# Two attention layers on one core: even exponentials of the second layer summed by accumulating transfers, five split steps, projections in half blocks

## The chip, the cores and the metric

The kernel runs on one core of a Trainium2 chip. A core has five engines with queues of their own: PE (TensorE, matrix products into PSUM), DVE (VectorE) and ACT (ScalarE) for elementwise work, POOL (GpSimd) for elementwise work and for issuing DMAs, and SP (SyncE), which here issues DMAs only. The metric is the device time of one execution in microseconds; lower is better. Times named "profiled" come from one execution that the hardware profiler recorded.

## The reference

Input is `x` of 4 images, 64 x 64 positions, 256 channels, fp32. Each image is 4096 tokens. Two self-attention layers follow one another, both without scaling of the scores and both over the whole image:

```
layer 0:  q = x@Wq+bq  k = x@Wk+bk  v = x@Wv+bv        (32, 32, 256 wide)
          x = gamma * softmax(q k^T) v + x
layer 1:  f = x@Wf+bf  g = x@Wg+bg  v = x@Wh+bh        (32, 32, 128 wide)
          x = x + (softmax(g f^T) v) @ Wo + bo
```

All of it is fp32; the kernel keeps fp32-like accuracy while it runs most products in the faster rounded form (`fp32r`) with values that are split into a high and a low part.

## The kernel before

The kernel works image by image: layer 0 of an image ("first"), then its layer 1 ("second"). No scores are ever stored: exponentials are used as they come, and the division by their sum is done at the end of a block of queries.

**First layer.** 16 blocks of 256 queries; each goes in 8 steps over four key tiles of 128 keys. A step has four score products into the PSUM buffer `st` (L505), two exponentials on ACT, `high` (L515, with a small bias, rounded) and `p` (L517), then `low = p - high` on DVE (L522) and `d`, a combination of low and high (L527). `products_first` (L536) multiplies high, low and d by three prepared forms of v: 24 matmuls 258 wide, which also produce the sum of exponentials.

**Second layer.** Eight blocks of 512 queries; each goes in 16 steps over two key tiles. Scores are two products 512 wide (L505). Most steps multiply `p` with `v` in plain fp32 ("whole", L557, two products); the steps with `i % 5 == 2`, that is 2, 7 and 12, are split: high, low and d by three forms of v, six products in fp32r at L557. The sum of the exponentials is kept on DVE in `p_sum` (128 x 1024): a copy at step 0 (L696), an add in each of the 15 others (L698). At the end of a block `end_second` takes the result from PSUM to `o` (L613, L614), folds `p_sum` to `sums` (L616), and four `output` units do the product with Wo (L624), the sum over partitions (L625), the reciprocal (L627), scaling and residual (L628), and the store (L630).

**Order.** The main loop's iteration n issues the scores of step n+2, some small units of other work, then the products of step n. The program's order is a priority; a scheduler decides what stands where in each engine's queue, and tile pools decide when a buffer is free: one score buffer (two PSUM banks), four accumulators, two side banks. In SBUF `p` has three buffers, tag `t` (high, and p of the second layer's split steps) two, `l` two, `d` one (in the second layer it holds `p_sum`), q two, k eight.

**Projections.** One unit list per block of 512 tokens: `transpose_unit` (32 x 32 squares loaded by DMA, turned on DVE at L381, xh on ACT at L387, xl on DVE at L388), `qk_unit` (four products 512 wide at L412, ACT and DVE work at L422 to L425, and a store to `qk_dram` at L428), and `v_unit` (L442, then `split_values` at L400 to L403 or a plain copy at L463). `load_k` and `load_q` (L472) bring the rows of k and q back in the layout that the scores want, as four DMAs of 32 rows each, issued from POOL. The units are spread evenly over a block's steps; layer 1's projections of an image run during its layer 0, the last of them in the first block of its layer 1, and the next image's layer-0 projections run during layer 1. In the first image's first block projections run beside the steps as early units, three blocks ahead.

Of the kernel before, what the change touches and what calls it, by code (L numbers as in the profile page):

```python
# [55 lines left out]
P = 128  # L57
QB = 512
# [4 lines left out]
EPS = 2.0**-12  # L63
AHEAD = 3

# [168 lines left out]
def fast_path(ctx: ExitStack, tc: tile.TileContext, x, w0, w1, wo, bo, gamma, out, off):  # L234
# [13 lines left out]
    split = [[l == 0 or i % 5 == 2 for i in range(NI[l])] for l in range(2)]  # L248
# [11 lines left out]
    def wide(tag, name, dtype=F32):  # L260
        return work.tile([P, 2 * QB], dtype, tag=tag, bufs={"d": 1, "p": 3}.get(tag, 2), name=name)
# [5 lines left out]
    def load_squares(key, tokens):  # L267

        turned[key] = []
        for c in range(NCC):  # L270
            t = work.tile([P, QB], F32, tag="squares", bufs=5, name=f"squares_{key[0]}_{key[1]}_{key[2]}_{c}")
            for a in range(P // S):
                ch = c * P + a * S
                nc.sync.dma_start(
                    t[a * S : (a + 1) * S, :].rearrange("j (b i) -> j b i", i=S),
                    tokens[:, ch : ch + S].rearrange("(b j) i -> j b i", j=S),
                )
            turned[key].append(t)

    def load_block(b, j):  # L280
        if b < B and j < NB:
            load_squares((b, 0, j), x[b, j * QB : (j + 1) * QB, :])


    x_nat = {}

    def load_first(j):
        if j < NB:
            x_nat[j] = []
            for n in range(j * NT, (j + 1) * NT):  # L290
                x_nat[j].append(data.tile([P, C], F32, tag="v1", bufs=V1, name=f"x_nat_{n}"))
                nc.sync.dma_start(x_nat[j][-1], x[0, n * P : (n + 1) * P, :])

    load_first(0)
    load_first(1)

# [7 lines left out]
    seen_v = const.tile([P, 2, B * NB, 2], F32, name="seen_v")  # L304
# [61 lines left out]
    xT, x_parts, k_t, v_t = {}, {}, {}, {}  # L366
    qk_dram, x1_dram, x1_res = {}, {}, {}
    q_t = {}


    def transpose_unit(b, l, j):
        def issue():
            xT[b, l, j] = data.tile([P, NCC, QB], F32, tag="xT", name=f"xT_{b}_{l}_{j}")
            for c in range(NCC):
                if b == l == 0:
                    ps = side_psum(f"psx_{j}_{c}")
                    for t in range(NT):
                        nc.tensor.transpose(ps[:, t * P : (t + 1) * P], x_nat[j][t][:, c * P : (c + 1) * P], ident)
                    nc.scalar.copy(xT[b, l, j][:, c, :], ps)
                else:  # L380
                    nc.vector.transpose(xT[b, l, j][:, c, :], turned[b, l, j][c])  # L381
            x_parts[b, l, j] = []
            for c in range(NCC):
                parts = [
                    work.tile([P, QB], F32R, tag="squares", bufs=5, name=f"x{what}_{b}_{l}_{j}_{c}") for what in "hl"
                ]
                nc.scalar.copy(parts[0], xT[b, l, j][:, c, :])  # L387
                nc.vector.tensor_sub(parts[1], xT[b, l, j][:, c, :], parts[0].bitcast(F32))  # L388
                x_parts[b, l, j].append(parts)
            if b == l == 0:  # L390
                load_first(j + 2)
            elif l == 0:
                load_block(b, j + 1)
            elif j == NB - 1:
                load_block(b + 1, 0)

        return issue

    def split_values(v, h, low, d, seen):
        nc.scalar.activation(h, v, AF.Copy, scale=1.0 - DOWN)  # L400
        nc.scalar.activation(low, v, AF.Abs, accum_out=seen)
        nc.vector.scalar_tensor_tensor(d, h.bitcast(F32), -1.0 - EPS, v, ALU.mult, ALU.add)
        nc.vector.scalar_tensor_tensor(low, d.bitcast(F32), 1.0 / EPS, h.bitcast(F32), ALU.mult, ALU.add)  # L403

    def project_units(b, l, j):
        key = (b, l, j)

        def qk_unit():
            ps = side_psum(f"psqk_{b}_{l}_{j}")
            for c in range(NCC):  # L410
                for n in range(2):
                    nc.tensor.matmul(  # L412
                        ps,
                        wqk[l][:, c, :],
                        x_parts[key][c][n],
                        start=(c == n == 0),
                        stop=(c == NCC - 1 and n == 1),
                    )
            whole = data.tile([2 * D, QB], F32, tag="qk", name=f"qk_{b}_{l}_{j}")
            parts = data.tile([P, QB], F32R, tag="qk_parts", name=f"qk_parts_{b}_{l}_{j}")  # L420
# [6 lines left out]
            qk_dram[key] = dram.tile([2, 2, D, QB], F32, name=f"qk_dram_{b}_{l}_{j}")  # L427
            nc.sync.dma_start(qk_dram[key].rearrange("h w d n -> (h w d) n"), parts.bitcast(F32))  # L428
            if b == l == 0:
                near = parts.rearrange("(h w d) n -> h w d n", h=2, w=2)  # L430
                load_k(b, l, j, near)
                if j == 0:
                    load_q(b, l, j, near)

        per = QB // CV[l]

        def v_unit(t0):
            def issue():
                ps = side_psum(f"psv_{b}_{l}_{j}_{t0}").rearrange("p (t c) -> p t c", c=CV[l])
                for t in range(per):  # L440
                    for c in range(NCC):
                        nc.tensor.matmul(  # L442
                            ps[:, t, :],
                            xT[key][:, c, (t0 + t) * P : (t0 + t + 1) * P],
                            wv[l][:, c, :],
                            start=(c == 0),
                            stop=(c == NCC - 1),
                        )
                tiles = slice(t0, t0 + per)
                seen = [seen_v[:, l, b * NB + j, n : n + 1] for n in range(2)]  # L450
                if l == 0:
                    split_values(ps, *(v0[j][what][:, tiles, :C] for what in ("h", "l", "d")), seen[t0 // per])
                    return
                for n in range(NT // G[1]):
                    i = j * NT // G[1] + n
                    v = ps[:, n * G[1] : (n + 1) * G[1], :]
                    if split[1][i]:
                        t = data.tile([P, 3, G[1], P], F32R, tag="v1_parts", bufs=sum(split[1]), name=f"v_{b}_{i}")
                        v_t[b, i] = {what: t[:, m] for m, what in enumerate(("h", "l", "d"))}
                        split_values(v, *v_t[b, i].values(), seen[n])  # L460
                    else:
                        v_t[b, i] = data.tile([P, G[1], P], F32, tag="v1", bufs=V1, name=f"v_{b}_{i}")
                        nc.scalar.copy(v_t[b, i], v)  # L463
                        nc.scalar.activation(v, v, AF.Abs, accum_out=seen[n])  # L464

            return issue

        return [transpose_unit(b, l, j), qk_unit] + [v_unit(t0) for t0 in range(0, NT, per)]

    def load_rows(dst, parts, which, halves):  # L470
        for n, h in enumerate(halves):
            nc.gpsimd.dma_start(dst[n * D : (n + 1) * D, :], parts[h, which])  # L472

    def load_q(b, l, j, parts=None):
        q_t[b, l, j] = data.tile([P, QB], F32R, tag="q", bufs=2, name=f"q_{b}_{l}_{j}")
        load_rows(q_t[b, l, j], qk_dram[b, l, j].bitcast(F32R) if parts is None else parts, 0, (0, 0, 1, 1))

    def load_k(b, l, j, parts=None):
        k_t[b, l, j] = data.tile([P, QB], F32R, tag="k", bufs=NB, name=f"k_{b}_{l}_{j}")
        load_rows(k_t[b, l, j], qk_dram[b, l, j].bitcast(F32R) if parts is None else parts, 1, (0, 1, 0, 1))  # L480
# [8 lines left out]
    class Step:  # L489
# [8 lines left out]
        def scores(self):  # L498
# [18 lines left out]
            nc.scalar.activation(self.p, s_flat, AF.Exp)  # L517

# [5 lines left out]
        def cut_both(self):  # L524
            if self.split:
                self.d = wide("d" if self.l == 0 else "l", f"d_{self.key}", F32R)
                nc.vector.scalar_tensor_tensor(  # L527
                    self.d, self.low.bitcast(F32), -1.0 / EPS, self.high.bitcast(F32), ALU.mult, ALU.add
                )

# [13 lines left out]
        def products_second(self, acc):  # L544
            v = v_t[self.b, self.i]
            some = [i for i in range(NI[1]) if split[1][i]]
            for p, v, which, first, last in (
                (
                    (self.high, v["h"], 0, self.i == some[0], False),
                    (self.low, v["l"], 0, False, self.i == some[-1]),  # L550
                    (self.d, v["d"], 1, self.first, self.last),
                )
                if self.split
                else ((self.p, v, 1, self.first, self.last),)
            ):
                for g in range(G[1]):
                    nc.tensor.matmul(  # L557
                        acc[which],
                        v[:, g, :],
# [6 lines left out]
    def end_first(b, j, acc):  # L566
# [11 lines left out]
        def residual(s):  # L578
            def issue():
# [11 lines left out]
                if part == QB // QB0 - 1 and s == NS - 1:  # L591
                    load_squares((b, 1, jj), x1_dram[b, jj])
# [14 lines left out]
    def end_second(b, j, acc, p_sum):  # L607
# [7 lines left out]
        sums = work.tile([P, QB], F32, tag="sums", bufs=1, name=f"sums_{key}")  # L615
# [181 lines left out]
```

## Time and profile before

| What | us |
|---|---|
| median of 3 runs (3223.26 to 3223.58) | 3223.3 |
| the profiled execution | 3222.18 |
| its span (granted clock 0.998) | 3220.4 |
| first-layer block, without and with a projection | 26.9 and 29.6 |
| the first block of all | 67.2 |
| second layer, images 0 to 2: block 0; block 1; a later block | 51.0 to 52.7; 40.36; 41.75 |
| second layer, image 3: block 0; block 1; a later block | 45.05; 35.78; 37.17 |
| image 3's last block to the end of PE's work | 48.05 |

A block's time is the distance between the first score products of two blocks in the timeline of PE. The second layer of images 0 to 2 also carries the projections of the next image; image 3 has none to carry. Where a line of the profile names a line number, as L557, it is that of the kernel before; `acc<-p,v` means that `acc` is written from `p` and `v`.

### The profile page before, as it was taken

What the parts mean: (1) busy time and instruction counts of PE and PEld (TensorE: products, weight loads), DVE (VectorE), ACT (ScalarE), POOL (GpSimd) and SP (SyncE); (2) the same over time, 40 slices, a digit from 0 to 9 for tenths busy, and PEclk for the clock granted to TensorE, in tenths of its full rate; (3) what the DMA queues carried; (4) which work ended last, traced back from release to release, by engine and by line L of the source; (5) the groups of instructions that cost most, each with busy time, mean ns of one, the idle gap of its engine ahead of it and who ended that gap; (6) DMA issues with size and microseconds to landing.
All of it is one profiled execution on the core that took longest, in us unless ns stands there. A gap on an engine that the chain in (4) does not pass through costs nothing. (4 is left out here: it accounts for less than half of the span.)

```text
span 3220.4 us, 51144 instructions
## 1 busy us (share of the span) xinstructions
PE 3166.5 (98%) x19460; PEld 2613.0 (81%) x19460; DVE 2691.5 (84%) x3181; ACT 1988.8 (62%) x2483; POOL 661.3 (21%) x784
## 2 busy tenths in 40 slices
PE   8999999999999999999999999999999999999998
PEld 7999997566799999655679999966558999995554
DVE  7888888888888888788888888878888888887776
ACT  6666666655566666565556666655555666665554
POOL 3222223000232222200022222310002222241000
PEclk9999999999999999999999999999999999999999
DMA  4111123221212112322121112232222211121110
GB/s 120 47 47 44 50 50 83 56 53 49 59 44 54 44 52 49 79 53 53 49 64 42 49 50 50 61 70 52 51 52 57 53 41 47 46 70 47 36 36 31
DMA packets 368653, 172.16 MB, mean 53 GB/s; under 512 B 257392, under 2 KB 343664, under 8 KB 368400
## 3 DMA queue, kind: packets, MB, share of 16 engines
q1 hardware_dynamic: 342528, 134.29, 16.0%
q0 software_dynamic: 24960, 34.18, 4.5%
q8 instruction: 157, 2.57, 0.3%
q14 instruction: 96, 0.79, 0.1%
q10 hardware_dynamic: 912, 0.33, 0.0%
HBM read 99.22 MB, written 67.11 MB: 52 GB/s over the span
## 5 line engine op out<-in xcount | busy, mean ns | idle before, releaser
L517 ACT ACTIVATE p<-st 128x1024 f32<-128x1024 f32 x1024 | 1044.5, 1020 | 393.6 <-PE st L505 369.5
L515 ACT ACTIVATE high<-st,down 128x1024 fp32r<-128x1024 f32 x608 | 678.8, 1116 | 683.6 <-PE st L505 572.7
L527 DVE SCALAR_TENSOR_TENSOR d<-low,high 128x1024 fp32r<-128x1024 f32 x608 | 761.2, 1252 | 208.3 <-PE acc L536 202.9
L522 DVE TENSOR_TENSOR low<-p,high 128x1024 fp32r<-128x1024 f32 x608 | 810.6, 1333 | 134.2 <-ACT p L517 134.2
L557 PE MATMUL acc<-p,v 128*128 128x512 f32 x1664 | 795.2, 597 | 0.0
L505 PE MATMUL st<-q,k 128*128 128x256 f32 (+1 forms) x3072 | 778.6, 361 | 8.4 <-ACT p L517 8.3
L698 DVE TENSOR_TENSOR p_sum<-p_sum,p 128x1024 f32<-128x1024 f32 x480 | 587.1, 1223 | 60.7 <-ACT p L517 47.5
L505 PEld LDWEIGHTS st<-q,k 128*128 128x128 f32 x3072 | 461.2, 189 | 210.7 <-ACT p L517 113.3
L536 PE MATMUL acc<-v0d,d 128*128 128x258 f32 x4096 | 591.7, 284 | 1.7 <-DVE d L527 1.6
L536 PE MATMUL acc<-v0h,high 128*128 128x258 f32 x4096 | 588.6, 283 | 1.6 <-ACT high L515 1.6
L536 PE MATMUL acc<-v0l,low 128*128 128x258 f32 x4096 | 587.0, 283 | 0.5 <-DVE low L522 0.5
L536 PEld LDWEIGHTS acc<-v0d,d 128*128 128x128 f32 x4096 | 533.1, 189 | 6.7 <-DVE d L527 3.6
L536 PEld LDWEIGHTS acc<-v0h,high 128*128 128x128 f32 x4096 | 534.1, 190 | 3.4 <-ACT high L515 2.0
L536 PEld LDWEIGHTS acc<-v0l,low 128*128 128x128 f32 x4096 | 532.7, 189 | 0.8 <-DVE low L522 0.7
L557 PEld LDWEIGHTS acc<-p,v 128*128 128x128 f32 x1664 | 308.4, 190 | 214.3 <-issue 184.7
L593 POOL TENSOR_TENSOR x_res<-x,bo 128x256 f32<-128x256 f32 x128 | 216.3, 1690 | 889.9 <-DVE g L583 482.0
L472 POOL DMA_DIRECT2D q<-qk_dram x252 | 123.9, 501 | 1166.1 <-PE st L505 1143.0
L676 POOL TENSOR_TENSOR x_res<-x_res,bv 128x256 f32<-128x256 f32 x128 | 189.6, 1482 | 114.4 <-DMA x_res<-in_x 85.0
L442 PE MATMUL psv<-wv,xT 128*128 128x128 f32 (+1 forms) x1024 | 194.8, 331 | 6.8 <-DVE qk L423 6.1
L442 PEld LDWEIGHTS psv<-wv,xT 128*128 128x128 f32 x1024 | 159.6, 192 | 29.8 <-DVE qk L423 8.5
L472 POOL DMA_DIRECT2D k<-qk_dram x224 | 109.6, 500 | 245.2 <-PE st L505 140.3
L388 DVE TENSOR_TENSOR xl<-xT,xh 128x512 fp32r<-128x512 f32 x128 | 87.1, 683 | 5.1 <-ACT xh L387 4.7
(96 smaller groups left out, 1701.9 us busy)
## 6 DMA issues: line engine op xcount, KB each, us to landing
x_res<-in_x SPq DMA_DIRECT2D x128, 128.0 KB, 2.2
qk_dram<-qk_parts SPq DMA_DIRECT2D x64, 256.0 KB, 2.1
x_dram<-x SPq DMA_DIRECT2D x128, 128.0 KB, 1.7
x_res<-x_res SPq DMA_DIRECT2D x128, 128.0 KB, 1.7
squares<-x_dram SPq DMA_DIRECT2D x256, 64.0 KB, 2.3
x_old<-x_res SPq DMA_DIRECT2D x128, 128.0 KB, 2.0
out<-x_old SPq DMA_DIRECT2D x128, 128.0 KB, 1.7
q<-qk_dram POOLq DMA_DIRECT2D x252, 64.0 KB, 2.1
```

Of the source, the lines that this page charges most:

```text
L442: nc.tensor.matmul(ps[:, t, :], xT[key][:, c, (t0 + t) * P : (t0 + t + 1) * P], wv[l][:, c, :], start=(c == 0), stop=(c == NCC - 1),)
L472: nc.gpsimd.dma_start(dst[n * D : (n + 1) * D, :], parts[h, which])
L505: nc.tensor.matmul(st[:, g, :], k_t[b, l, kt // NT][:, kt % NT * P : (kt % NT + 1) * P], q_t[b, l, j * n // QB][:, q0 : q0 + n], start=Tru ...
L515: nc.scalar.activation(self.high, s_flat, AF.Exp, bias=down)
L517: nc.scalar.activation(self.p, s_flat, AF.Exp)
L522: nc.vector.tensor_sub(self.low, self.p, self.high.bitcast(F32))
L527: nc.vector.scalar_tensor_tensor(self.d, self.low.bitcast(F32), -1.0 / EPS, self.high.bitcast(F32), ALU.mult, ALU.add)
L536: nc.tensor.matmul(acc[2 * s + which][:, :W], p[:, g * QB0 + s * P : g * QB0 + (s + 1) * P], v0[self.i][v][:, g, :], start=self.first and ...
L557: nc.tensor.matmul(acc[which], v[:, g, :], p[:, g * QB : (g + 1) * QB], start=first and g == 0, stop=last and g == G[1] - 1,)
L593: nc.gpsimd.tensor_add(x_old[s], x_new[s], bo_sb)
L676: nc.gpsimd.tensor_add(x_res[b, j][t], x_res[b, j][t], bv)
L698: nc.vector.tensor_add(p_sum, p_sum, s.p)
```

## The change

Four things are done, all around the second layer and the projections:

1. `SPLIT1`: the second layer's split steps are 1, 4, 7, 10 and 13 (five of 16) instead of 2, 7 and 12.
2. `MOVED_SUMS`: the exponentials of the eight even steps are summed by DMAs that POOL issues. Step 0's p is copied into a tile `moved_sums` (tag `e`, one buffer), those of 2, 4, ... 14 are added to it by a DMA with `accum_op=add`; each DMA has 128 rows of 4096 bytes. DVE adds only odd steps (`add_up`; step 1 is a copy), and `end_second` adds `moved_sums` to `p_sum`.
3. Projections go by half blocks of 256 tokens: squares, xT, xh, xl, qk_parts are half as wide or hold both channel halves in one tile; psqk is four matmuls of 256 per half; each half is written to `qk_dram` by itself. In the first image's lead, xT, its parts and qk_parts share the five buffers of `v1_parts`, and k rows are loaded half by half.
4. `plan()` puts the units at given steps instead of an even spread: layer 1's halves in layer 0's blocks from 2 on, the last two halves at steps 0, 2, 3 and 6, 8, 9 of the second layer's block 0, the next image's halves seven steps apart.

`UP` is `1/EPS` as a constant. The core of the diff:

```diff
+SPLIT1 = (1, 4, 7, 10, 13)
+MOVED_SUMS = (0, 2, 4, 6, 8, 10, 12, 14)
...
-    split = [[l == 0 or i % 5 == 2 for i in range(NI[l])] for l in range(2)]
+    NH = N // QB0
+    split = [[l == 0 or i in SPLIT1 for i in range(NI[l])] for l in range(2)]
...
-        return work.tile([P, 2 * QB], dtype, tag=tag, bufs={"d": 1, "p": 3}.get(tag, 2), name=name)
+        return work.tile([P, 2 * QB], dtype, tag=tag, bufs={"d": 1, "e": 1, "p": 3}.get(tag, 2), name=name)
...
             self.p = wide("t" if self.split and l == 1 else "p", f"p_{self.key}")
             nc.scalar.activation(self.p, s_flat, AF.Exp)
+            if l == 1 and i in MOVED_SUMS:
+                if i == MOVED_SUMS[0]:
+                    moved_sums[b, j] = wide("e", f"p_sum_moved_{b}_{j}")
+                    nc.gpsimd.dma_start(moved_sums[b, j], self.p)
+                else:
+                    nc.gpsimd.dma_start(moved_sums[b, j], self.p, accum_op=ALU.add)
...
+        def add_up(self, p_sum):
+            if self.l == 0 or self.i in MOVED_SUMS:
+                return
+            if self.i == 1:
+                nc.vector.tensor_copy(p_sum, self.p)
+            else:
+                nc.vector.tensor_add(p_sum, p_sum, self.p)
...
         sums = work.tile([P, QB], F32, tag="sums", bufs=1, name=f"sums_{key}")
+        nc.vector.tensor_add(p_sum, p_sum, moved_sums[b, j])
         nc.vector.tensor_add(sums, p_sum[:, :QB], p_sum[:, QB:])
...
-        turned[key] = []
+        t = work.tile([P, NCC, QB0], F32, tag="squares", bufs=1, name="squares_" + "_".join(map(str, key)))
...
+            lead = b == l == 0
+            tag = "v1_parts" if lead else "xT"
+            xT[key] = data.tile([P, NCC, QB0], F32, tag=tag, bufs=LEAD_BUFS if lead else 1, name=f"xT_{b}_{l}_{h}")
...
+            if part == 0:
+                qk_dram[b, l, j] = dram.tile([2, 2, D, QB], F32, name=f"qk_dram_{b}_{l}_{j}")
+            nc.sync.dma_start(qk_dram[b, l, j].rearrange("h w d n -> (h w d) n")[:, cols], parts.bitcast(F32))
+            halves[b, l, j] = part + 1
...
+    def plan(b, l, j, ends):
+
+        units = {}
+
+        def put(i, *some):
+            units.setdefault(i, []).extend(some)
+
+        if l == 0:
+
+            if j >= 2:
+                t, qk, v = project_units(b, 1, j - 2)
+                put(0, t), put(4, qk), put(5, v)
+            for n, u in enumerate(ends):
+                put(1 + n, u)
+            return units
+        if j == 0:
+            for n, u in enumerate(ends):
+                put(1 + n, u)
+            for n, h in enumerate((NH - 2, NH - 1)):
+                t, qk, v = project_units(b, 1, h)
+                put(6 * n, t), put(6 * n + 2, qk), put(6 * n + 3, v)
+        else:
+            for n, u in enumerate(ends):
+                put(1 + n, u)
+        if b + 1 < B:
+            for h in range(NH):
+                i = 10 + 7 * h - j * NI[1]
+                for n, u in zip((0, 2, 3), project_units(b + 1, 0, h)):
+                    if 0 <= i + n < NI[1]:
+                        put(i + n, u)
+        return units
...
-        pace = NI[l] - (5 if l == 1 else 1)
-        upto = min(len(units), -(-len(units) * (s.i + 1) // pace))
-        todo = units[done:upto]
-        done = upto
+        s.add_up(p_sum)
+        todo = units.get(s.i, [])
...
-        while keys and keys[0] in qk_dram and (keys[0][:2] == (b, l) or keys[0][2] < over):
+        while keys and halves.get(keys[0]) == 2 and (keys[0][:2] == (b, l) or keys[0][2] < over):
             load_k(*keys.pop(0))
```

## The prediction

> **What bounds the kernel now.** I read the page first (busy shares, chain, groups), then the table of waits, then windows and timelines of single blocks of the second layer.
>
> ```profile
> PE 3166.5 (98%) x19460; PEld 2613.0 (81%) x19460; DVE 2691.5 (84%) x3181; ACT 1988.8 (62%) x2483; POOL 661.3 (21%) x784
> L557 PE MATMUL acc<-p,v 128*128 128x512 f32 x1664 | 795.2, 597 | 0.0
> L698 DVE TENSOR_TENSOR p_sum<-p_sum,p 128x1024 f32<-128x1024 f32 x480 | 587.1, 1223 | 60.7 <-ACT p L517 47.5
> k<-qk_dram POOLq DMA_DIRECT2D x224, 64.0 KB, 2.1
> ```
>
> TensorE (PE) is busy 98% of the span; VectorE (DVE) follows with 84%, 587 us of it the adds that this change halves. GpSimd (POOL) has room. So time goes only with PE work or with the few PE waits. The windows of three second-layer blocks (us, then busy PE, PEld, DVE, ACT, POOL, clock, DMA share, GB/s) show where the waits are: the first block of image 2, a later block of image 2, a block of image 3.
>
> ```profile
> 2107.60:2154.90 47.30, 41.62 (x134) 23.77 (x132) 36.85 (x43) 26.19 (x39) 5.47 (x6) 0.96 0.34 73
> 2237.00:2278.80 41.80, 41.55 (x141) 25.02 (x139) 35.52 (x44) 24.63 (x31) 2.01 (x5) 1.00 0.21 51
> 3015.70:3052.80 37.10, 36.79 (x119) 21.18 (x118) 29.19 (x34) 19.94 (x21) 1.88 (x5) 1.00 0.12 36
> ```
>
> Later blocks are full. The first block of an image has holes of 5.7 us, and its keys' load on POOL waits 23.43 us for the projection to reach memory:
>
> ```profile
> 2138.38 1.98 POOL L472 DMA_DIRECT2D k<-qk_dram  x4 [23.43 <-DMA qk_dram<-qk_parts]
> ...
> 2140.25 1.18 PE L557 MATMUL acc<-d,v 128*128 128x512 f32 x2 [1.54 <-DVE d L527]
> ...
> 2148.83 1.99 PE L442 MATMUL psv<-wv,xT 128*128 128x256 f32 x8 [1.84 <-DVE qk L423]
> ...
> 2153.00 0.72 PE L505 MATMUL st<-q,k 128*128 128x512 f32 x2 [1.71 <-ACT p L517]
> ```
>
> A split step is not free of waits either. Timeline of DVE and PE around step 12 of an image-3 block:
>
> ```profile
> 3046.94 1.22 DVE L522 TENSOR_TENSOR low<-p,high 128x1024 fp32r<-128x1024 f32 x1 [1.96 <-ACT p L517]
> 3048.09 1.22 DVE L698 TENSOR_TENSOR p_sum<-p_sum,p 128x1024 f32<-128x1024 f32 x1
> 3049.22 1.22 DVE L527 SCALAR_TENSOR_TENSOR d<-low,high 128x1024 fp32r<-128x1024 f32 x1
> ...
> 3050.49 0.73 PE L557 MATMUL acc<-d,v 128*128 128x512 f32 x2 [0.31 <-DVE d L527]
> ```
>
> An add sits between low and d and makes d late.
>
> **What the Trainium skill says.** "FP8 and Floating Point Precision", TensorE Precision Notes: true fp32 takes four passes. The trace agrees: successive unsplit steps start 2.18 us apart, 0.46 of it scores, so their two p·v matmuls take 1.72 us where two rounded ones of the same width take 0.46, a ratio of 3.7. "DMA: Bandwidth & Descriptors", Rules for kernel authors: an accumulating transfer is issued from GpSimd only, and another access to the same bytes waits for its semaphore; so the eight transfers of a block are a serial chain. No accumulating transfer is in the trace of before. "Collectives: The Full Stack", the bandwidth ceiling, says an add inside a transfer needs two reads for each write and so runs at about half a copy's rate; nothing here shows it.
>
> **The change part by part.** Sums start from the profiled execution, 3222.2 us (span 3220.4 plus 1.8 around it), 1.1 under the median of 3223.3.
>
> *Split steps.* Two more per block, 32 blocks: 64 steps. Unsplit: 2.18 us with scores; split: 8 x 0.23 = 1.845. So 64 x 0.335 = 21.4 us off PE. Not all arrives. An image-3 block takes 37.17 us (period between first scores); ideal is 13 x 2.18 + 3 x 1.845 + 2.28 (four output products of 0.57) = 36.16, so before loses 1.0, of it about 0.65 at step 12. The chain of a split step is scores, exp 1.11, exp 1.02, low 1.22, d 1.22: with hand-offs d is ready 5.25 us after the scores' start, 6.4 with an add between, and PE wants it at 5.8. After: 11 x 2.18 + 5 x 1.845 + 2.28 = 35.49. Odd steps keep their adds, and the compiled order on DVE still has add 7 and add 13 between low and d of steps 7 and 13. I put 0.5 at step 7, 1.35 at step 13 (d, and the single score buffer with two exponentials ahead of the last scores), 0.2 elsewhere: 37.5, that is +0.35 on an image-3 block. In images 0 to 2 a block has 41.75; ideal is 4.4 higher (3.46 psv + 0.96 psqk) and the projection's matmuls lie in the same holes, so I take 39.9 + 1.3 = 41.2: -0.55. 21 such blocks (two to eight) give -11.5, seven of image 3 +2.5.
>
> *The moved sums.* Seven adds and a copy leave DVE per block, one add of both sums comes in (L649 of after): net about -8 x 1.22 + 1.22 plus two lows and two ds, 4.9: DVE goes from 27.3 to 23.6 us per block. DVE isn't the bound, so this is worth only what waits it shortens. In place come 256 POOL transfers of 512 KB. Each waits for the one before. Their unknown cost T: k's 64 KB loads take 2.1 us from issue to landing with two packets of 0.1 per DMA engine, so 1.9 fixed; 512 KB is 8 rows of 4096 B per engine, at 159 ns per such packet on this queue 1.26, twice for two reads: T = 4.4. The skill's software path ("DMA: Bandwidth & Descriptors", Anatomy of one DMA) prices 2.0 us + bytes/436e3, an estimate of 4.4 for two reads, 3.2 for the copy. I take 4.6 with POOL's hand-off. Lower end 3.4 (reads of both operands side by side), upper end 6.5 (read, add and write one after the other). The block's chain is copy 3.2 + 7T + DVE's final add 1.6 = 37.0 at 4.6, against 37.5 and 41.2: it just fits, so I cost it at nothing in images 0 to 2 and 0 to 4 us in image 3. What hides it is that p has three buffers and each p's transfer has two steps (4.4 us or so) before its buffer is wanted. If the cover is gone ACT's exp waits (p of step 5 for transfer 0, high of 7 for transfer 4, and so on), then scores, then PE. Queued behind a waiting transfer on POOL are q's loads of a later block, which have a block to spare, in block 0 of an image the residual adds, and in block 7 k's loads for the next image.
>
> *Half blocks and fixed places.* Per projected block 8 psqk matmuls of 256 instead of 4 of 512: 0.96 instead of 0.93. Small DMAs double (squares, qk_dram; SP's queue has slack, transfers take 2 us and are issued half blocks ahead): nothing. What it buys is the start of a second-layer image: block 1's period and the projection taken away, block 0 of the four images loses 5.2 + 6.85 + 6.85 + 3.85 = 22.7 us against a steady one. After, only two halves remain for it, at steps 0 to 3 and 6 to 9 rather than to step 11, and the k rows of the last half are needed for scores of step 15 at step 13: ready 4 to 5 steps after qk at step 8, with 1 for projection chain, 2.1 for writing and 2.1 + 2 for loading. So I leave 1.6 each, 6.4, and gain 16; block 0's steady part moves by 3 x -0.55 + 0.35 = -1.3 like the others. Bounds: 8 to 20.
>
> *Start and end.* The first block of all takes 67.2 us against 26.9, of which PE's projections explain about 46. Now POOL issues 64 k loads of 0.5 us in it where it issued 32 (16 us more of a queue that gates the scores), and xT, its parts and qk_parts share a ring of five buffers; on the other side all work starts after half a block's input. I take +1, bounds -6 and +15. The end has one more DVE add in the tail, +1.2, and 2 for a transfer chain that lags in image 3.
>
> Sum: -11.5 + 2.5 - 16 - 1.3 + 1 + 1.2 + 2 = -22.1. That is a profiled execution of 3200.1; the median stood 1.1 higher, 3201.
>
> **The rivals.**
> A. The transfers are too slow (ends slower than before). The place is POOL's chain within a second-layer block, the price 8 us per block for each us of T (7 transfers and the copy), and it decides above T of about 5.1: there 7T + 4.8 = 40.5, +3.3 on the eight image-3 blocks (+27, which eats the -11.5 and -16) and nothing yet on the others. At T = 5.5 a block is 43.3: +1.5 on 24 blocks, +6 on eight, less the 16 to 18 at the starts: 3223 + 36 + 48 - 17 = 3290. At 6.5 it is 50.3: about +300. For it: no such transfer was measured here, each needs issue, landing and semaphore in series. Against it: POOL is 21% busy and its queue moves 4.5%.
> B. DVE, with 3.7 us less per block, gets d ready in time everywhere, so blocks come to 35.7 and 40.1: -1.65 on 24 and -1.5 on eight, -51, and -16 at the starts: about 3156. For it: low waits 134 us in all for p and adds fill those places. Against: add 7 and add 13 are still in between, and exp is the earlier link.
> C. Waits of the score buffer and d eat all of the split's gain (blocks +0.4 on both kinds, +13), the first block costs 8, and only part of the start stall goes (-16): within 0.2%, 3220.
>
> **How the numbers follow.** Forecast 0.50, A 0.33, B 0.10, C 0.07. The forecast's own range is 3182 to 3219 (starts 8 to 20, first block -6 to 15, blocks +-0.3). The range must reach into A: cut at T = 5.5 it leaves about a third to half of A out; below, 3165 leaves out B's better half. So 3165 to 3305. A measurement of this kernel can tell 0.2%, 6.4 us, from no change. Faster: forecast 0.49 and B 0.10, with little off for edges, 0.59; same 0.07; slower A 0.33 and a little of C, 0.34.
>
> **What would show it.** Accumulating transfers from issue to landing: under 5 us right, above A. Periods of 41.2 (images 0 to 2) and 37.5 (image 3); 39.1 or more there says A. DVE's add before sums waiting on a DMA for microseconds, and exp p waiting on a DMA, are A's marks. Block 0 of images 1 and 2 at about 46 instead of 52.6. d's waits at steps 7 and 13 on PE. First block 67 to 69. I am wrong if the transfers share their engines' time with the squares' small packets (16% of the queue share) and T varies, or if the half-block loads make k late at every start.

## The result and the profile after

The changed kernel takes 3330.4 us (median of 4 runs, 3327.6 to 3333.6) where the kernel before took 3223.4 beside it: a ratio of 1.033, 95% interval 1.032 to 1.035. It is slower by 107 us, outside the predicted range, and on the side of rival A. The page of the changed kernel, first part, then groups, then queues and DMA issues (issue to landing in us last):

```profile
PE 3195.1 (96%) x19844; PEld 2658.5 (80%) x19844; DVE 2605.9 (78%) x3229; ACT 2063.8 (62%) x2675; POOL 876.7 (26%) x1076
...
L545 POOL DMA_DIRECT2D p_sum_moved<-p x224 | 196.7, 878 | 942.0 <-ACT p L539 291.2
...
L649 DVE TENSOR_TENSOR p_sum<-p_sum,p_sum_moved 128x1024 f32<-128x1024 f32 x32 | 39.2, 1226 | 126.6 <-DMA p_sum_moved<-p 126.6
...
p_sum_moved<-p POOLq DMA_DIRECT2D x256, 512.0 KB, 4.9
```

The busy shares give no warning: PE went from 98% to 96%, DVE from 84% to 78%, ACT stays at 62%. POOL rose from 21% to 26%, which looks harmless. What gives it away is the group of L649: DVE's add of the two sums waits for the last transfer at the end of every one of 32 blocks, 126.6 us in all. The windows of one block of image 2 and two of image 3 (columns as before):

```profile
2278.10:2321.00 42.90, 42.56 (x153) 26.77 (x152) 31.90 (x44) 27.00 (x37) 8.48 (x12) 1.00 0.70 147
3089.90:3132.50 42.60, 38.07 (x124) 21.52 (x123) 25.54 (x31) 22.13 (x23) 8.63 (x12) 1.00 0.59 130
3132.50:3174.60 42.10, 38.08 (x124) 21.57 (x123) 25.58 (x31) 22.10 (x23) 8.62 (x12) 1.00 0.60 131
```

Image 3 is the clear case: 42.3 us a block for 38.1 of busy time on PE, where before it was 37.1 for 36.8. (By the prediction's own sum the products of a block fell from 36.2 to 35.5 us, so the 38.1 holds time in which PE was slowed too.) No engine fills the block, and the DMA engines are busy for only 0.60 of it. The block is a chain, and POOL's timeline shows it (start, duration, and in brackets the idle time ahead and what ended it):

```profile
3047.75 0.87 POOL L545 DMA_DIRECT2D p_sum_moved<-p  x1 [4.20 <-ACT p L539]
3048.28 2.33 POOL L490 DMA_DIRECT2D q<-qk_dram  x4
3054.81 0.56 POOL L543 DMA_DIRECT2D p_sum_moved<-p  x1 [4.19 <-ACT p L539]
3058.26 0.88 POOL L545 DMA_DIRECT2D p_sum_moved<-p  x1 [2.89 <-DMA p_sum_moved<-p]
3063.52 0.87 POOL L545 DMA_DIRECT2D p_sum_moved<-p  x1 [4.38 <-DMA p_sum_moved<-p]
3068.90 0.86 POOL L545 DMA_DIRECT2D p_sum_moved<-p  x1 [4.51 <-DMA p_sum_moved<-p]
3074.73 0.86 POOL L545 DMA_DIRECT2D p_sum_moved<-p  x1 [4.97 <-ACT p L539]
3080.16 0.86 POOL L545 DMA_DIRECT2D p_sum_moved<-p  x1 [4.57 <-ACT p L539]
3085.19 0.86 POOL L545 DMA_DIRECT2D p_sum_moved<-p  x1 [4.16 <-issue]
3090.25 0.86 POOL L545 DMA_DIRECT2D p_sum_moved<-p  x1 [4.20 <-ACT p L539]
```

From the copy at 3054.81 on, every issue follows its predecessor by 3.45 (the copy) and then 5.0 to 5.8 us, in all 35.4 to the last issue; the last transfer needs 5.5 more to land. In this case the releaser's name tells less than the distance: "ACT p" is the exponential that came last by the profile, in a step that was itself waiting. The landing is what counts: in the whole trace an accumulating transfer lands 4.9 us (median; 4.5 at the least) after its issue begins, and the next is issued 0.52 us (least; median 0.54) after that landing, so that from issue to issue the median is 5.4. The other end of the chain is on DVE:

```profile
3046.96 1.23 DVE L565 TENSOR_TENSOR p_sum<-p_sum,p 128x1024 f32<-128x1024 f32 x1 [0.20 <-ACT p L539]
3053.00 1.23 DVE L649 TENSOR_TENSOR p_sum<-p_sum,p_sum_moved 128x1024 f32<-128x1024 f32 x1 [4.82 <-DMA p_sum_moved<-p]
3054.26 0.69 DVE L650 TENSOR_TENSOR sums<-p_sum 128x512 f32<-128x512 f32 x1
3054.87 0.74 DVE L647 TENSOR_TENSOR o<-o,acc 128x256 f32<-128x256 f32 x2
3055.53 1.22 DVE L550 TENSOR_TENSOR low<-p,high 128x1024 fp32r<-128x1024 f32 x1
```

The transfer issued at 3047.75 lands just before 3053.0; DVE has stood still for 4.8 us, and only after L649 may the next block's copy overwrite the single `e` buffer, at 3054.81. Behind L649 in DVE's queue stands the next block's first `low`. So the chain closes over block borders, and it also reaches into the next image's first layer, where PE waits for that `low`:

```profile
881.44 1.34 PE L572 MATMUL acc<-v0l,low 128*128 128x258 f32 x8 [3.27 <-DVE low L550]
```

The spans differ by 105.4 us, and the distances between the first scores of blocks say where: second layer of images 0 to 2, +13.6, +15.2, +15.2; of image 3 up to PE's last product, +40.2; the first first-layer blocks of images 1 to 3, +15.1; the start, +4.2; the end after PE's last product, +1.8. These are 105.3 of the 105.4 us.

A part of it is a follow-up of the chain. In the profiled run the granted clock of PE was 0.5 in eleven stretches of 3.4 or 6.8 us, 48 us in all, the start and the end of the run aside; in the kernel before there were two, 6.8 us together. Each begins within 1.3 us of the end of a PE wait of 1.5 to 4.0 us. An estimate from these figures: up to half of the 41 us more, some 20 us of the loss, is PE at the lower clock after waits.

The long blocks of images 0 to 2 are blocks 4 and 7 (46.5 to 48.8 us; the other later blocks 42.2 to 45.5). The timeline of DVE and ACT at the start of image 0's block 4 shows a second way in which the chain holds them:

```profile
696.20 1.23 DVE L649 TENSOR_TENSOR p_sum<-p_sum,p_sum_moved 128x1024 f32<-128x1024 f32 x1 [4.17 <-DMA p_sum_moved<-p]
697.34 0.70 DVE L391 STREAM_TRANSPOSE xT<-squares 128x512 f32<-128x512 f32 x1
...
698.08 0.62 ACT L404 CAST xh<-xT 128x512 fp32r<-128x512 f32 x1 [4.62 <-DVE xT L391]
...
698.60 1.11 ACT L537 ACTIVATE high<-st,down 128x1024 fp32r<-128x1024 f32 x1
```

The next image's projection stands behind L649 on DVE, ACT waits for it, and the block's next exponentials stand behind that on ACT. Block 4 of images 1 and 2 looks the same, and in block 7 ACT waits 1.9 to 3.4 us for `qk` (L443), which stands behind L649 too. That this makes these blocks long is a reading of the timelines; no run changed it alone.

### The profile page after: what moved, and what is told of

It is laid out like the page before. It is cut to its first block, busy times and chain, and to the rows that moved or that the text cites. A ratio compares the mean times of both kernels' runs of the same rounds, so it can differ in the third digit from the quotient of the medians.

```text
span 3325.8 us, 53634 instructions
## 1 busy us (share of the span) xinstructions
PE 3195.1 (96%) x19844; PEld 2658.5 (80%) x19844; DVE 2605.9 (78%) x3229; ACT 2063.8 (62%) x2675; POOL 876.7 (26%) x1076
## 5 line engine op out<-in xcount | busy, mean ns | idle before, releaser
L537 ACT ACTIVATE high<-st,down 128x1024 fp32r<-128x1024 f32 x672 | 749.9, 1116 | 776.6 <-PE st L527 605.2
L550 DVE TENSOR_TENSOR low<-p,high 128x1024 fp32r<-128x1024 f32 x672 | 884.6, 1316 | 265.6 <-ACT p L539 265.0
L555 DVE SCALAR_TENSOR_TENSOR d<-low,high 128x1024 fp32r<-128x1024 f32 x672 | 849.0, 1263 | 186.7 <-PE acc L572 175.0
L527 PE MATMUL st<-q,k 128*128 128x256 f32 (+1 forms) x3072 | 740.0, 349 | 46.2 <-ACT p L539 35.5
L590 PE MATMUL acc<-p,v 128*128 128x512 f32 x1408 | 675.5, 601 | 0.0
L545 POOL DMA_DIRECT2D p_sum_moved<-p x224 | 196.7, 878 | 942.0 <-ACT p L539 291.2
L626 POOL TENSOR_TENSOR x_res<-x,bo 128x256 f32<-128x256 f32 x128 | 201.5, 1574 | 832.8 <-DVE x L618 829.7
L590 PEld LDWEIGHTS acc<-p,v 128*128 128x128 f32 x1408 | 261.3, 191 | 188.1 <-issue 165.6
L565 DVE TENSOR_TENSOR p_sum<-p_sum,p 128x1024 f32<-128x1024 f32 x224 | 273.2, 1219 | 19.8 <-ACT p L539 18.5
L649 DVE TENSOR_TENSOR p_sum<-p_sum,p_sum_moved 128x1024 f32<-128x1024 f32 x32 | 39.2, 1226 | 126.6 <-DMA p_sum_moved<-p 126.6
```

The costliest lines, as they stand in the source:

```text
L527: nc.tensor.matmul(st[:, g, :], k_t[b, l, kt // NT][:, kt % NT * P : (kt % NT + 1) * P], q_t[b, l, j * n // QB][:, q0 : q0 + n], start=Tru ...
L537: nc.scalar.activation(self.high, s_flat, AF.Exp, bias=down)
L545: nc.gpsimd.dma_start(moved_sums[b, j], self.p, accum_op=ALU.add)
L550: nc.vector.tensor_sub(self.low, self.p, self.high.bitcast(F32))
L555: nc.vector.scalar_tensor_tensor(self.d, self.low.bitcast(F32), -UP, self.high.bitcast(F32), ALU.mult, ALU.add)
L565: nc.vector.tensor_add(p_sum, p_sum, self.p)
```

## Experiments

Times are medians; the kernel before, run beside them, had 3222.5 to 3223.9. "A block" is a block of image 3 in the steady state unless said otherwise: 37.17 us before, about 42.3 in the changed kernel.

**All sums back on DVE.** `add_up` copies at step 0, and the add of the moved sum goes.

```diff
-MOVED_SUMS = (0, 2, 4, 6, 8, 10, 12, 14)
+MOVED_SUMS = ()
```

> The changed kernel with all 16 sums of a block back on DVE, everything else kept. Transfer chain (a block's period in the second layer is 7 times 5.2 to 5.6 us plus the copy and DVE's final add): without it image-3 blocks fall from 42.5 to about 37.5, the others from 43 to 47 down to about 41.2, the first first-layer block of images 1 to 3 from 34.3 to 29.5; 3195 to 3215 us in all. Split waits (five split steps with one score buffer and late d hold the blocks): blocks stay above 42, 3290 or more. Traffic (the moved bytes slow the engines' SBUF accesses): the same 3195 to 3215, so this run does not tell it from the chain.

3217.6 us, ratio 0.998 (0.9975 to 0.9993), just above the 3195 to 3215 that the chain would give. A block takes 38.03, blocks of images 0 to 2 41.0 to 42.7, the first first-layer block of images 1 to 3 29.1 (34.2 to 35.0 with the transfers). So the transfers cost 113 us, and the rest of the change is worth 6, not the 25 that I had summed for it (the sum of -22.1 has 3.2 of loss in it for the moved sums). Split waits as the main cause are out.

**Copies in place of adds.** The same 256 transfers in the same chain, without the add.

```diff
-                    nc.gpsimd.dma_start(moved_sums[b, j], self.p, accum_op=ALU.add)
+                    nc.gpsimd.dma_start(moved_sums[b, j], self.p)
```

> All eight transfers of a block are plain copies into the same tile, one after the other, so the tile ends up with the last even step's exponentials only and the even steps' sum is left out; issues, waits and written bytes stay. Transfer chain: a copy takes 2.9 us to landing and 0.53 to the next issue, 8 x 3.4 = 27 us, hidden under a block of 37 or 41; image-3 blocks about 37.3, in all 3185 to 3210. Split waits: stays at about 3320. Traffic: a third of the bytes (one of two reads) is gone, so about a third of the loss: about 3290.

3212.7 us, 3 above the chain's span. The DMA view of this kernel:

```profile
p_sum_moved<-p POOLq DMA_DIRECT2D x256, 512.0 KB, 3.0
```

8 x (3.0 + 0.5) = 28 us goes under any block, and the whole loss is gone although issues, waits and written bytes are all there. The chain is borne out; traffic, which should have kept two thirds of the loss, is not. But the adds themselves are gone too, and POOL is held 0.53 us for an issue instead of 0.87, so the next two runs, which keep adds, are needed beside this one. A block took 38.3, a us above the expected 37.3, as in the run before: that is the splits' share (below).

**Half-wide transfers, two chains.**

```diff
+                for g in range(2):
+                    cols = self.p[:, g * QB : (g + 1) * QB]
...
+                        nc.gpsimd.dma_start(moved_sums[b, j, g], cols, accum_op=ALU.add)
```

> Each moved sum is two transfers of half the columns into two tiles, so two chains of 256 KB transfers run side by side; same bytes and work, twice the issues. If T is mostly fixed latency (about 2 us plus 0.5 of hand-off, the rest by size), a half transfer lands in about 3.5, the chain is about 8 x 4 = 32 us and hidden: 3200 to 3225. If T is the engines' rate for the bytes, both halves together take what one took, 4.9, and two issues of 0.87 each come on top: 3330 or more. Split waits: 3330.

3233.4 us, much nearer to the fixed-latency value, 8 us above its end. The least time of an accumulating transfer fell from 4.5 to 3.25 us, of the copy from 2.86 to 2.26. If time grows in line with size, 4.5 - 3.25 = 1.25 for half the bytes makes 2.5 us by size and 2.0 fixed for a whole one. In the run the median of the half adds was 4.0, so part of the gain is lost; where two meet is the likely place. All adds and all bytes are still there, and all but 16 us of the 113 are gone: this is the strongest run against traffic.

**Four moved sums.** `MOVED_SUMS = (0, 4, 8, 12)`.

> Only steps 0, 4, 8 and 12 are moved, DVE adds the other twelve. Transfer chain: copy 3.4 + 3 x 5.5 + 1.6 = 21.5 us, well hidden under a block: 3195 to 3215, the same as with all sums on DVE or a few us less. Traffic: half of the loss remains, about 3265. Split waits: 3310 or more.

3211.6 us, as the chain says; with three of seven accumulating transfers kept, none of the loss is. A block takes 37.98: four sums fewer on DVE, with one add back at the end, are worth next to nothing against all 16 (38.03).

**Nine moved sums.** `MOVED_SUMS` with 15 added: the suspected cost enlarged.

> Step 15's sum is moved too, a ninth transfer at the end of each block. Transfer chain: it lengthens the chain of 32 blocks by one T of 5.3 to 5.5, less the DVE add of 1.2 that goes: 32 x 4.3 to 5.5, so 3465 to 3505 us. If the blocks were held by splits or by traffic, one transfer more costs at most 32 x 0.6 or so: about 3350.

3490.5 us (two runs): +160 for 32 transfers, 5.0 us each, inside the expected span. This is the price of one more link of the chain.

These runs settle the slowdown. The next ones ask why the rest gained 6 us only, and what five splits are worth.

**Three splits, sums on DVE.** Split steps 2, 7, 12 as before the change; the lead keeps its five buffers.

```diff
-SPLIT1 = (1, 4, 7, 10, 13)
+SPLIT1 = (2, 7, 12)
```

> All sums on DVE and the split steps 2, 7, 12 as in the kernel before; half blocks, fixed places and the five-buffer lead of the changed kernel stay. With five splits and sums on DVE the median was 3217.6, an image-3 block 38.04. If two more splits cost time instead of saving it (late d or score buffer): image-3 blocks about 37.2, in all 3195 to 3212. If five splits do save part of their 21 us: 3220 to 3235. Either way block 0 of images 1 and 2 at 43 to 46, which is what the half blocks bring.

3217.9 us and a block of 38.03: the same as with five. So the 64 further split steps brought nothing; and with the same split steps as the kernel before, a block is 0.86 longer. Neither expectation foresaw both. In this kernel's timeline of DVE and PE both later split steps (7 and 12) show the late `d` that the kernel before had at step 12 only:

```profile
3062.29 1.22 DVE L565 TENSOR_TENSOR p_sum<-p_sum,p 128x1024 f32<-128x1024 f32 x1
3063.43 1.22 DVE L555 SCALAR_TENSOR_TENSOR d<-low,high 128x1024 fp32r<-128x1024 f32 x1
...
3064.70 0.74 PE L590 MATMUL acc<-d,v 128*128 128x512 f32 x2 [0.32 <-DVE d L555]
...
3075.93 0.73 PE L590 MATMUL acc<-d,v 128*128 128x512 f32 x2 [0.32 <-DVE d L555]
```

The kernel before had an output product (0.57 us of PE) between the splits' scores and their products, since its units were spread over the block; at its step 12, whose `d` was late, there was none. `plan()` puts all four at steps 1 to 4. That this makes the 0.86 is a reading of the two timelines; with three splits it was not run.

**Four splits, sums on DVE.** `SPLIT1 = (1, 5, 9, 13)`.

> All sums on DVE, four split steps 1, 5, 9, 13. Score buffer: four steps need 3 x 1.85 + 2.8 = 8.35 us of the buffer against PE's 3 x 2.18 + 1.845 = 8.39, so PE can just follow; image-3 blocks 36.7 to 37.1 and about 3190 to 3200. Late d: one late d of about 0.65 per split, 4 x 0.65 over an ideal of 35.83, 38.4 at most, 37.5 at least, 3205 to 3220.

3210.5 us, a block 37.69: inside the span of late d, above that of the score buffer. Taken alone it speaks for late d as the limit; the next run shows that this isn't enough.

**The splits' own sums moved.** The add that stands between low and d is that of the split step itself, so moving just those takes it away.

```diff
-MOVED_SUMS = (0, 2, 4, 6, 8, 10, 12, 14)
+MOVED_SUMS = (1, 4, 7, 10, 13)
```

> The five split steps' own sums (1, 4, 7, 10, 13) are the moved ones, so no add stands between low and d on DVE; 3.4 + 4 x 5.5 = 25 us of chain, hidden. With four moved sums the second half of an image-3 block ran at 6.89 us per three steps, 0.35 of it PE's wait for d. Late d (the add between low and d costs the split's gain): the wait goes, three steps take 6.2 to 6.35, an image-3 block 36.3, in all about 3165 to 3180. Score buffer (one buffer, emptied by two exponentials in a split step, 1.85 + 1.85 + 2.8 = 6.5 per three steps, more than PE's 6.2): three steps stay at 6.5 to 6.7, a block at 37.0 to 37.5, 3190 to 3200.

3203.8 us, ratio 0.994 (0.993 to 0.996). The profile shows no wait of PE for d any more (about 1.0 us a block with four moved sums), yet three steps take 6.7 to 6.8 us (6.89 before) and a block 37.47, not 36.3. Late d accounts for about 0.5 us of a block; something else is nearly as late. The block lies in the score buffer's span, the total 4 us above it.

**High from p.** In the second layer p is exponentiated first, and high made from p, not from the scores.

```diff
             if self.split:
                 self.high = wide("t", f"high_{self.key}", F32R)
-                nc.scalar.activation(self.high, s_flat, AF.Exp, bias=down)
+                if l == 0:
+                    nc.scalar.activation(self.high, s_flat, AF.Exp, bias=down)
             self.p = wide("t" if self.split and l == 1 else "p", f"p_{self.key}")
             nc.scalar.activation(self.p, s_flat, AF.Exp)
+            if self.split and l == 1:
+                nc.scalar.activation(self.high, self.p, AF.Copy, scale=1.0 - DOWN)
```

> The split steps' own sums are moved, and in the second layer p is exponentiated first and high is made from p in SBUF, so that the score buffer is free after one exponential in every step. With own sums moved alone the median was 3203.8, three steps took 6.83 us and an image-3 block 37.47. Score buffer: 3 x 1.85 = 5.6 us is now under PE's 6.2, so three steps take 6.2 to 6.4 and an image-3 block 35.8 to 36.3, images 0 to 2 at 40 to 40.6; 32 blocks by 1.2 make about 3165. Late high and d: high comes 1.1 us later, low and d with it, and PE waits for them in the score buffer's place; three steps stay at 6.8 or more, 3200 or more.

With the own sums moved: 3199.0 us, a block 37.30 and three steps 6.7; the expected 36.3 was missed by a us. PE's timeline of this kernel:

```profile
3051.16 0.62 PE L593 MATMUL acc<-low,v 128*128 128x512 f32 x2
3051.97 0.49 PE L527 MATMUL st<-q,k 128*128 128x512 f32 x1 [0.19 <-ACT p L540]
3052.30 0.65 PE L593 MATMUL acc<-d,v 128*128 128x512 f32 x2
```

The scores now stand ahead of d in most split steps and wait for the exponential of the step before. That one waits for its own scores in the one buffer, and these for an exponential that stands right behind `high` in ACT's queue. And d is later than it was. DVE's timeline:

```profile
3048.67 1.22 DVE L553 TENSOR_TENSOR low<-p,high 128x1024 fp32r<-128x1024 f32 x1 [2.07 <-ACT high L542]
3049.82 1.22 DVE L568 TENSOR_TENSOR p_sum<-p_sum,p 128x1024 f32<-128x1024 f32 x1
3050.95 1.22 DVE L558 SCALAR_TENSOR_TENSOR d<-low,high 128x1024 fp32r<-128x1024 f32 x1
```

An add, that of the next step, is between low and d again. At steps 7, 10 and 13 of an image-3 block d is ready 6.3 to 6.9 us after the step's scores start, where the run with own sums moved had 5.3 to 5.7. The rival expectation, late high and d, is nearer to this run than the score buffer is.

> All sums on DVE and high made from p, so that only the score buffer's hold is changed against the run with sums on DVE (3217.6 us, image-3 block 38.04). Score buffer alone as the limit: 36.5 or less a block, about 3170. Late d: the add stays between low and d, and high is 1.1 us later, so PE's wait for d grows from 0.35 to about 1 a split step; 38.0 to 39.5 a block, 3215 to 3250.

With all sums on DVE: 3199.2 us, ratio 0.992 (0.990 to 0.994); a block 36.77, that is 1.27 below the same kernel with high from the scores. The total fell by 18 us, less than half of the 47 that the score buffer alone should have brought. The expectation for late d doesn't hold as it was put, for the edit changed DVE's order as well (step 10 of an image-3 block):

```profile
3053.55 1.23 DVE L568 TENSOR_TENSOR p_sum<-p_sum,p 128x1024 f32<-128x1024 f32 x1 [0.54 <-ACT p L540]
3054.69 1.22 DVE L553 TENSOR_TENSOR low<-p,high 128x1024 fp32r<-128x1024 f32 x1
3056.02 1.23 DVE L558 SCALAR_TENSOR_TENSOR d<-low,high 128x1024 fp32r<-128x1024 f32 x1
```

The split step's own add needs only p and now goes ahead of low. At some split steps the next step's add comes between low and d in its place, at this one none does. So at steps 7, 10 and 13 d is ready 5.5 to 6.7 us after the scores' start, against 6.3 to 6.7 with high from the scores: no later. The run therefore says nothing against late d. What the two runs show together is that the same edit brings 1.27 a block where d comes no later and 0.17 where d comes about 1.2 us later. That fits a limit of two parts, the hold of the score buffer and d, but no run changed the buffer alone.

**A ring of six in the lead.** Sums on DVE, `LEAD_BUFS = 6`.

> All sums on DVE, and the ring that the first image's projections share has six buffers instead of five. With five the first block took 80.3 us and the median was 3217.6. Ring as the limit of the start: the first block falls to 68 to 74, in all 3205 to 3212. Small pieces as the limit (hand-offs of 16 half blocks one after the other): it stays at 78 to 82 and 3215 to 3220.

3214.8 us against 3217.6. The first block takes 74.1 instead of 80.3, but begins at 22.1 instead of 17.6 us: the end of the first block comes 1.7 earlier. The ring matters to the first block's length and hardly to the whole; neither expectation held in full.

**Outputs at the split steps.** Sums on DVE, high from p, and in blocks 1 to 7 of an image:

```diff
             for n, u in enumerate(ends):
-                put(1 + n, u)
+                put(1 + 3 * n, u)
```

> All sums on DVE, high made from p, and a block's four output units at the split steps 1, 4, 7, 10 instead of steps 1 to 4 (blocks 1 to 7 of an image). Against 3199.2 us and an image-3 block of 36.77 with the outputs at steps 1 to 4. Bunching theory (an output product beside a split step gives high, low and d the time they lack; steps 7, 10 and 13 had none, which is also why three splits with fixed places took 38.03 a block where the kernel before, with its spread units, took 37.17): 36.0 to 36.4 a block, 28 blocks by 0.4 to 0.7, so 3179 to 3188. If the places of the outputs don't matter: 36.7 to 36.8, 3197 to 3201.

3183.8 us, ratio 0.9875 (0.986 to 0.989), a block 36.20, both inside the expected spans. The places of the outputs matter, and this version is the fastest of all, about 1.2% below the kernel before: it has the half blocks and five splits of the change, high made from p, and no accumulating transfer.

## Why the prediction was wrong

The step that failed is "The moved sums": "T = 4.4 ... I take 4.6 with POOL's hand-off ... it just fits, so I cost it at nothing" in images 0 to 2, with 2 us in the sum for image 3. The mechanism, a serial chain, was named rightly; its link was sized at 4.6 us and measured 5.4 (median from issue to issue), so that the chain did not fit under a block and cost 113 us.

- **T.** The transfer itself was estimated well: 1.9 fixed and 2.5 by size against 2.0 and 2.5 by the half-wide run, 4.4 against a least time of 4.5. The sum left out two things: the median is 4.9, not 4.5 (other traffic is a likely reason, not a tried one), and from landing to the next issue 0.52 us pass where I gave 0.2. Seven times the missing 0.8 is 5.6 us of a chain that had 0.5 to spare in image 3 and 4.2 in the others.
- **The point of decision.** I wrote that rival A decides above 5.1. That held, and so did its formula for a block: 7 x 5.4 + 4.8 = 42.6 for image 3, measured 42.3. Its marks are all there: besides DVE's 126.6 us before L649, ACT's exponentials wait 60.5 us in all for `p_sum_moved`. The price that I put beside it, 8 us a block per us of T, doesn't follow from the formula, which gives 7. A term with so steep a price and an estimate half a us below its edge should not have been the likeliest case; the choice of the value inside its bounds was the error, not the list of bounds.
- **Rival A's 3290 at T = 5.5** was 40 us short. Its own terms make about 23 us for the second layer of images 0 to 2 and 44 for image 3; measured are 44 and 40. It left out the projection's hold on ACT and DVE in blocks 4 and 7, L649's hold on the next image's first layer (+15), the start (+4) and the end (+2).
- **The skill's half rate for an add.** One packet of 4096 bytes took 161 ns (median) in the copies of step 0 and 338 in the adds, so just under half the rate. "Collectives: The Full Stack", the bandwidth ceiling, says it of a reduction between cores; inside this core the trace agrees.
- **Split steps: -11.5 in images 0 to 2 and +2.5 in image 3.** With sums on DVE these blocks did not gain: 0.2 us longer each over blocks 1 to 7 of image 1, and 0.87 longer in image 3. The parts named (d, the score buffer) were right in kind as far as the runs tell, their size was not. In the kernel before three split steps took (37.17 - 13 x 2.18 - 2.28) / 3 = 2.18 us each on average, just what a whole step takes, so a saving of 0.335 per step was not being realised even there; I had read the lost 1.0 us mostly as a fault of step 12.
- **Add 7 and add 13 between low and d.** True of the order, but with the own sums moved a block is only 0.5 shorter than with four other sums moved.
- **Fixed places.** I gave the bunching of the outputs no cost. It cost 0.57 a block with high from p (36.77 to 36.20), as much as the 0.5 that I put at step 7.
- **Image starts: -16.** With sums on DVE block 0 came to 43.5 in images 0 to 2 (51.0 to 52.7 before) and 42.7 in image 3 (45.05), 28 us in all, of which 4.4 came back in block 1. The direction was right and the term too small by a third; half blocks and fixed places were not tried apart. In the changed kernel the chain hid half of it: block 0 came to 45.6 to 48.4, 14 us in all.
- **Start and end.** The first block was not 67 to 69 us long but 78.3, and began 6.7 earlier; its end came 4.4 us later (6.5 with sums on DVE), where I had +1 within -6 to +15. The end after PE's last product took 1.8 longer, and 3.0 with all sums on DVE, which has no such add at the end: so the add that I costed at 1.2 is not the reason, which stays open.
- **Rival B** (DVE's relief brings the blocks to 35.7): out. With half the sums moved as copies, under a chain that fits, a block took 38.3, and with a quarter moved 37.98, against 38.03. Only moving the splits' own adds helped, by 0.5.
- **Rival C's sum.** Its terms, +13, +8 and -16, make 3228, not 3220. The kernel with sums on DVE, which comes nearest to what C describes, took 3217.6.

## What to carry to other kernels

Work that is moved off an engine onto a DMA has to be priced as a chain: when each transfer must wait for the one before, add landing and hand-off, multiply by the number between two points that can't slip, and compare with the period, whatever the busy shares say. Here the sum came within 0.5 us of the period and the real chain was 5 us over it; when it is that close, do fewer links, or shorter ones side by side. And before buying faster steps, look at what a fast step takes now: here a split step already cost as much as a whole one on average. Making high from p and placing the output products beside the split steps brought 34 us.

## What the runs showed of the hardware

An accumulating SBUF-to-SBUF transfer of 128 rows of 4096 bytes takes 4.5 us at the least and 4.9 in the middle from the start of its issue to its landing, a copy of the same size 2.9; halved, 3.25 and 2.3 at the least. Its packets of 4096 bytes take 338 ns each (median), a copy's 161. POOL is held 0.87 us for issuing the add, 0.55 for the copy. From a landing to the next issue that waits for it 0.52 us pass. While these transfers ran in the second layer, ACT's and DVE's wide operations kept their durations: exponentials of p 1.02 us with and without them, d 1.214 and 1.215. The other loads that POOL issues did not: those of k landed after 3.2 us (median), 2.2 with all sums on DVE.
